# Two scan steps to one GpSimd product, and the next B rows queued one step earlier

## The chip, the cores and the metric

The kernel runs on one core of a Trainium2 chip. Its five engines work side by side, each through its own queue in order: TensorE (PE in the profile, PEld for its weight loads), VectorE (DVE), ScalarE (ACT), GpSimd (POOL) and SyncE (SP), which issues most of the DMAs. The metric is device time in microseconds (us). The median of four runs before the change is 2376.67 us (2375.16 to 2380.18).

## The reference

Input is x of shape (4, 256, 32, 32), 1024 positions for each of four images. A metaformer layer is computed: a channel norm, then four Mamba branches of 64 channels each (inner width 128, 16 states), gates and depthwise convolutions along the positions, attention with eight heads, a second norm with a 3x3 depthwise convolution, and after that a mixture of eight experts with two experts a token. What matters here is the selective scan, for each image, branch, inner channel d and state s:

```
dA = jnp.exp(dt[..., None] * A)
dBu = (dt * u)[..., None] * Bm[:, :, None, :]
def step(h, inp):
    dA_t, dBu_t, C_t = inp
    h = dA_t * h + dBu_t
    return (h, jnp.einsum('bds,bs->bd', h, C_t))
```

The scan runs over the 1024 positions; y is the sum over the 16 states of h times C.

## The kernel before

Images b, branches n and halves h of 512 positions make 4 x 4 x 2 = 32 *parts*, in that order (`parts`, L678). A part has 128 x 16 recurrences of length 512. They are laid on 128 partitions in 16 *steps*: step i = 4q + g takes the channels 32g to 32g+31 and the states 4q to 4q+3. Four steps with the same q are a *block* here; they share B rows and C rows.

For one step, ACT makes the decay dA = exp(dt x A) from `dts` (`decay`, L604), DVE makes the inflow dBu = (dt u) x B (`inflow`, L612), with B's rows in a PSUM bank, and DVE runs the recurrence (`step`, L623) with one scan instruction, out of PSUM and SBUF into an SBUF tile hs. In the first half (h = 0) POOL copies hs's last column into `last` (L627), from which the second half's scan starts. POOL then multiplies hs by C's rows in place (L628). PE sums the four states of a channel with a matmul against `quads` into yp (`sums_of`, L634), one block at a time.

B's rows, spread over 128 partitions, are also made by PE: `spread_b` (L592) issues four matmuls (eight instructions in the profile) with a column of the projection broadcast as weights; it needs u and a PSUM bank. The last step of a block writes its inflow over those rows. C's rows come by DMA (`spread_c`, L586), as dt and dt u do for the four channel groups (`spread_dt`, L567).

`scan` (L710) emits one step. Its order is written out by hand: at the block's third step (g == 2) the next block's `spread_b`; then things of the previous part (`before`: last sums at step 1, `gather` at 3, `project_out` at 6, `add_skip` at 8), things of the next part (`behind`: its dt at steps 0 to 5, its DMAs at 10 to 14, its first `spread_b` at 14), and the next branch's projections (`group`: for instance `project_u` at steps 9 and 10 of the first half); then, at g == 1, `sums_of` for the block before; then the decay three steps ahead, the inflow one step ahead, and the step itself. Each engine does its work in the order in which it was emitted.

After each step comes one `beat`, which advances side tasks by a little: the next image's norm, the convolutions of the image before (`convolutions`, during the first half of an image's parts), and after the fourth part of an image attention of the image before, in which the scan stands still until attention's last tiles. `resume` then takes the scan up again while `joined` (the attention output and fc products, L378), `around` and `sent_off` (routing, with POOL's row scatters at L1692) run in the beats. Expert tiles are a side task from the last part on, and the rest of them follow.

SBUF tiles come from pools of numbered slots: `act4` has 7 slots of 4 KB a partition (u, z, the norm's rows and others), `act2` has 17 of 2 KB (decays, hs, softplus's two, y, and in attention the exponentials e, four a key tile). PSUM has eight banks of 512 columns, one pool for all. A new tile takes a freed slot, and its first writer waits for the old tile's last users.

Of the kernel before, what the change touches and what calls it, by code (L numbers as in the profile page):

```python
# [9 lines left out]
F32 = mybir.dt.float32  # L10
AF = mybir.ActivationFunctionType
ALU = mybir.AluOpType
AX = mybir.AxisListType

P = 128
# [4 lines left out]
HALF = 512  # L20
# [52 lines left out]
def network(  # L73
# [27 lines left out]
    nc = tc.nc  # L101
# [42 lines left out]
    with tc.tile_pool(name="w_conv", bufs=1) as wp, tc.tile_pool(  # L144
        name="act8", bufs=8
    ) as act8, tc.tile_pool(name="act4", bufs=7) as act4, tc.tile_pool(
        name="act2", bufs=17
    ) as act2, tc.tile_pool(name="steps", bufs=2) as actd, tc.tile_pool(
        name="steps4", bufs=6
    ) as acts, tc.tile_pool(name="rows", bufs=3) as actc, tc.tile_pool(  # L150
        name="small", bufs=1
    ) as small, tc.tile_pool(
        name="spread", bufs=2, space=bass.MemoryType.DRAM
# [126 lines left out]
        GD, GS = DIN // 32, DS // 4  # L280
# [71 lines left out]
        def a4(name):  # L352
            return act4.tile([P, N], F32, tag="a4", name=name)

        def a2(name, rows=P):
            return act2.tile([rows, HALF], F32, tag="a2", name=name)
# [144 lines left out]
        T = {}  # L501
# [114 lines left out]
        def step(b, n, h, i):  # L616
            q, g = divmod(i, GD)
            dBu = T.pop((b, n, h, "dBu", i))
            hs = T[b, n, h, "hs", i] = a2(f"hs_{b}_{n}_{h}_{i}")
            if h == 0 and i == 0:  # L620
                T[b, n, "last"] = small.tile([P, NSTEP], F32, tag="last", name=f"last_{b}_{n}", bufs=2)
            last = T[b, n, "last"][:, i : i + 1]
            nc.vector.tensor_tensor_scan(  # L623
                hs, T[b, n, h, "dA", i], dBu, 0.0 if h == 0 else last, ALU.mult, ALU.add
            )
            if h == 0:
                nc.gpsimd.tensor_copy(last, hs[:, HALF - 1 : HALF])  # L627
            nc.gpsimd.tensor_tensor(hs, hs, T[b, n, h, "cs", q], ALU.mult)  # L628

# [21 lines left out]
        def add_skip(b, n, h):  # L651
# [14 lines left out]
            0: [(project_dt,)], 2: [(softplus,)], 4: [(sum_dt,)], 5: [(times_u,)],  # L666
            10: [(spread_dt, 0)], 11: [(spread_dt, 1)], 13: [(spread_dt, 2), (spread_c, 0)],
            14: [(spread_b, 0), (spread_dt, 3)],
        }
# [40 lines left out]
        def scan(at, i, stop):  # L710

            b, n, h = parts[at]
            q, g = divmod(i, GD)
            if g == 2 and q + 1 < GS:
                spread_b(b, n, h, q + 1)
# [216 lines left out]
        def attention(b):  # L932
# [12 lines left out]
            def logits(g, h, kt):  # L945
# [3 lines left out]
                for i in range(4):  # L949
# [4 lines left out]
                    if shifted:  # L954
# [3 lines left out]
                        )  # L958
                es = [a2(f"e_{b}_{g}_{h}_{kt}_{i}") for i in range(4)]
                for i in range(4):  # L960
# [455 lines left out]
class Experts:  # L1416
# [11 lines left out]
    T = 256  # L1428
# [649 lines left out]
```

## Time and profile before

| | before |
|---|---|
| median of four runs | 2376.67 us |
| the profiled execution | 2375.53 us, span 2373.8 us |
| PE, DVE, ACT, POOL busy | 2086.4, 1579.4, 1188.0, 1102.1 us |
| L628, products with C | 512 of 1327 ns |
| L627, copies of the last column | 256 of 236 ns |
| L623, scans | 512, 1207 ns for h = 0 and 1268 ns for h = 1 |
| L612, inflows | 512 of 674 to 678 ns |

In lines of the waits the columns are: engine, line and output that waited, what it waited for, us in total, times, longest. In lines of groups they are: line, engine, operation, output and inputs, shapes, count, then busy us and mean ns, then idle time before them and who ended it. In lines in order of time: start, duration, engine, line, operation, count, and in brackets the idle time before. PE's instructions are pipelined, so a group of them counts as busy a little beyond its last issue.

### The profile page before, as it was taken

What the parts mean: (1) busy time and instruction counts of PE and PEld (TensorE: products, weight loads), DVE (VectorE), ACT (ScalarE), POOL (GpSimd) and SP (SyncE); (2) the same over time, 40 slices, a digit from 0 to 9 for tenths busy, and PEclk for the clock granted to TensorE, in tenths of its full rate; (3) what the DMA queues carried; (4) which work ended last, traced back from release to release, by engine and by line L of the source; (5) the groups of instructions that cost most, each with busy time, mean ns of one, the idle gap of its engine ahead of it and who ended that gap; (6) DMA issues with size and microseconds to landing.
All of it is one profiled execution on the core that took longest, in us unless ns stands there. A gap on an engine that the chain in (4) does not pass through costs nothing. (4 is left out here: it accounts for less than half of the span.)

```text
span 2373.8 us, 28321 instructions
## 1 busy us (share of the span) xinstructions
PE 2086.4 (88%) x8810; PEld 926.9 (39%) x8810; DVE 1579.4 (67%) x2255; ACT 1188.0 (50%) x2013; POOL 1102.1 (46%) x1185
## 2 busy tenths in 40 slices
PE   7778877999887899987779999768999999999995
PEld 2112111332211232322113323205652578788884
DVE  3989999756798888689797876987344164211111
ACT  3554555477656368764264775415258443222221
POOL 0778888612688650565876115571140012422221
PEclk7988998999998999998789999679999999999997
DMA  2454443301343330233433102443340155777764
GB/s 85 118 141 110 110 109 76 88 26 36 87 104 93 74 75 28 57 87 94 115 78 77 32 23 54 104 141 115 80 134 1 43 182 171 230 203 196 197 190 153
DMA packets 155022, 244.33 MB, mean 103 GB/s; under 512 B 34212, under 2 KB 103492, under 8 KB 154856
## 3 DMA queue, kind: packets, MB, share of 16 engines
q1 hardware_dynamic: 135680, 217.07, 32.9%
q0 software_dynamic: 13264, 17.85, 3.9%
q10 hardware_dynamic: 5912, 7.45, 0.9%
q8 instruction: 74, 1.21, 0.2%
q14 instruction: 92, 0.75, 0.1%
HBM read 141.17 MB, written 33.98 MB: 74 GB/s over the span
## 5 line engine op out<-in xcount | busy, mean ns | idle before, releaser
L628 POOL TENSOR_TENSOR hs<-hs,cs 128x512 f32<-128x512 f32 x512 | 678.1, 1327 | 157.4 <-DVE hs L623 92.0
L634 PE MATMUL yp<-hs,quads 128*32 128x512 f32 x1024 | 374.1, 664 | 180.1 <-POOL hs L628 132.5
L604 ACT ACTIVATE dA<-dts,A 128x512 f32<-128x512 f32 x512 | 341.1, 712 | 179.6 <-DMA dts<-dt 127.2
L1945 POOL DMA_INDIRECT Y<-ys,dest x70 | 114.0, 1629 | 535.5 <-DVE ys L1939 528.8
L612 DVE TENSOR_TENSOR dBu<-dts,bs 128x512 f32<-128x512 f32 x384 | 259.9, 678 | 141.5 <-PE bs L596 133.9
L961 ACT ACTIVATE e<-st 128x512 f32<-128x512 f32 x512 | 263.1, 607 | 81.4 <-PE st L951 68.6
L1924 ACT ACTIVATE hs<-h,b 128x256 f32<-128x256 f32 x280 | 115.8, 472 | 341.3 <-PE h L1919 151.7
L1929 PE MATMUL y<-w,hs 128*128 128x256 f32 x1120 | 258.2, 382 | 6.4 <-ACT hs L1924 6.4
L1919 PE MATMUL h<-xT,w 128*128 128x256 f32 x1120 | 252.6, 382 | 1.8 <-DVE xT L1897 1.8
L623 DVE TENSOR_TENSOR_SCAN hs<-dA,last,dBu 128x512 f32<-128x512 f32 x192 | 243.4, 1268 | 0.3
L623 DVE TENSOR_TENSOR_SCAN hs<-dA,dBu 128x512 f32<-128x512 f32 x192 | 231.7, 1207 | 11.7 <-PE av L971 9.8
L627 POOL COPY last<-hs 128x1 f32<-128x1 f32 x256 | 60.4, 236 | 369.2 <-DVE hs L623 364.5
L634 PEld LDWEIGHTS yp<-hs,quads 128*32 128x32 f32 x1024 | 51.7, 112 | 455.1 <-POOL hs L628 319.0
L1919 PEld LDWEIGHTS h<-xT,w 128*128 128x128 f32 x1120 | 213.6, 191 | 39.8 <-issue 7.8
L1929 PEld LDWEIGHTS y<-w,hs 128*128 128x128 f32 x1120 | 211.3, 192 | 42.6 <-issue 8.2
L596 PE MATMUL bs<-u,xpwT_s 128*32 128x512 f32 x1024 | 225.2, 685 | 0.0
L1897 DVE COPY xT<-xp 128x512 f32<-128x512 f32 x35 | 24.2, 691 | 289.4 <-PE xp L1896 289.4
L1003 DVE TENSOR_TENSOR e<-e,e 128x512 f32<-128x512 f32 x256 | 169.7, 724 | 64.6 <-ACT e L961 30.2
L951 PE MATMUL st<-qk 32*128 32x512 f32 x1024 | 192.1, 651 | 7.7 <-ACT e L961 6.1
L993 PE MATMUL av<-e,v 128*32 128x512 f32 x1024 | 144.9, 627 | 0.0
L512 PE MATMUL up<-xn,inwk 64*128 64x512 f32 x256 | 127.7, 641 | 3.4 <-DVE hs L623 3.4
L951 PEld LDWEIGHTS st<-qk 32*128 32x128 f32 x1024 | 68.8, 186 | 129.6 <-issue 87.5
(279 smaller groups left out, 2691.6 us busy)
## 6 DMA issues: line engine op xcount, KB each, us to landing
w<-in_W_dram SPq DMA_DIRECT2D x136, 512.0 KB
dts<-dt SPq DMA_DIRECT2D x512, 128.0 KB
cs<-cd SPq DMA_DIRECT2D x512, 64.0 KB
xs<-XS SPq DMA_DIRECT2D x35, 260.0 KB
b<-in_b_dram SPq DMA_DIRECT2D x35, 128.0 KB
xn<-in_x_dram SPq DMA_DIRECT2D x8, 512.0 KB
XL<-xl SPq DMA_DIRECT2D x8, 512.0 KB
xl<-XL SPq DMA_DIRECT2D x4, 1024.0 KB
```

What stands on the lines that cost most here:

```text
L596: nc.tensor.matmul(bs[r], xpwT_s[:, n, s : s + 1].to_broadcast([P, 32]), T[b, n, "u"][:, half(h)], start=True, stop=True,)
L604: nc.scalar.activation(dA, T[b, n, h, "dts", g][:, 0, :], AF.Exp, scale=A[:, g, n, q : q + 1])
L612: nc.vector.tensor_tensor(dBu, T[b, n, h, "dts", g][:, 1, :], T[b, n, h, "bs", q], ALU.mult)
L623: nc.vector.tensor_tensor_scan(hs, T[b, n, h, "dA", i], dBu, 0.0 if h == 0 else last, ALU.mult, ALU.add)
L628: nc.gpsimd.tensor_tensor(hs, hs, T[b, n, h, "cs", q], ALU.mult)
L634: nc.tensor.matmul(T[b, n, h, "yp"][ts(g, 32)], quads, T[b, n, h, "hs", q * GD + g], start=(q == 0), stop=(q == GS - 1),)
L951: nc.tensor.matmul(sts[i], k[r, ts(kt, P)], q[r, half(h)], start=True, stop=not shifted)
L961: nc.scalar.activation(es[i], sts[i], AF.Exp, scale=1.0 / HD**0.5)
L993: nc.tensor.matmul(accs[0][ts(i, HD)], v8[:, kt, ts(4 * g + i, HD)], es[i], start=(kt == 0), stop=(kt == NK - 1),)
L1003: nc.vector.tensor_tensor(first[i], first[i], es[i], ALU.add)
L1919: nc.tensor.matmul(hp[:, i, :], w1(c, k), xT[:, c, :], start=(c == 0), stop=(c == NC2 - 1))
L1929: nc.tensor.matmul(yp[:, ts(t, C)], hs[:, k, ts(t, P)], w2(k), start=(k == 0), stop=(k == NHC - 1))
```

## The change

The two steps 2k and 2k+1 write their states into the two halves of one 4 KB tile from `act4`. At the even step only the scan is issued. At the odd step POOL copies the two last columns with one instruction (first half only) and multiplies both states by C's rows with one instruction of 1024 columns, in which the C rows are read twice. `spread_b` for the next block is emitted at the block's second step, ahead of that step's `sums_of`; a part's first `spread_b` at step 13 of the part before, ahead of the sums there. `act4` has 11 slots, `act2` 9. In attention the exponentials of even key tiles lie in pairs in `act4`.

```
-    ) as act8, tc.tile_pool(name="act4", bufs=7) as act4, tc.tile_pool(
-        name="act2", bufs=17
+    ) as act8, tc.tile_pool(name="act4", bufs=11) as act4, tc.tile_pool(
+        name="act2", bufs=9
...
+        def pair(name):
+            return act4.tile([P, 2, HALF], F32, tag="a4", name=name)
...
-            hs = T[b, n, h, "hs", i] = a2(f"hs_{b}_{n}_{h}_{i}")
+            if i % 2 == 0:
+                T[b, n, h, "two"] = pair(f"hs_{b}_{n}_{h}_{i}")
+            two = T[b, n, h, "two"]
+            hs = T[b, n, h, "hs", i] = two[:, i % 2, :]
...
+            if i % 2 == 0:
+                return
             if h == 0:
-                nc.gpsimd.tensor_copy(last, hs[:, HALF - 1 : HALF])
-            nc.gpsimd.tensor_tensor(hs, hs, T[b, n, h, "cs", q], ALU.mult)
+                nc.gpsimd.tensor_copy(
+                    T[b, n, "last"][:, i - 1 : i + 1].rearrange("p (g a) -> p g a", a=1),
+                    two[:, :, HALF - 1 : HALF],
+                )
+            nc.gpsimd.tensor_tensor(
+                two, two,
+                T[b, n, h, "cs", q].rearrange("p (a x) -> p a x", a=1).to_broadcast([P, 2, HALF]),
+                ALU.mult,
+            )
...
-            10: [(spread_dt, 0)], 11: [(spread_dt, 1)], 13: [(spread_dt, 2), (spread_c, 0)],
-            14: [(spread_b, 0), (spread_dt, 3)],
+            10: [(spread_dt, 0)], 11: [(spread_dt, 1)],
+            13: [(spread_b, 0), (spread_dt, 2), (spread_c, 0)], 14: [(spread_dt, 3)],
...
-            if g == 2 and q + 1 < GS:
+            if g == 1 and q + 1 < GS:
                 spread_b(b, n, h, q + 1)
...
-                es = [a2(f"e_{b}_{g}_{h}_{kt}_{i}") for i in range(4)]
+                if kt % 2 == 0:
+                    two = [pair(f"e_{b}_{g}_{h}_{kt}_{i}") for i in range(2)]
+                    es = [two[i // 2][:, i % 2, :] for i in range(4)]
+                else:
+                    es = [a2(f"e_{b}_{g}_{h}_{kt}_{i}") for i in range(4)]
```

## The prediction

> **What bounds the kernel now.** I read the page's slices first, then the waits by total, then windows by stage, then DVE's instructions in order of time where it had waited. In this execution the scan's first step starts at 59.8 us, its last ends at 1590, and the mixture of experts fills the rest.
>
> ```profile
> span 2373.8 us, 28321 instructions
> PE   7778877999887899987779999768999999999995
> DVE  3989999756798888689797876987344164211111
> POOL 0778888612688650565876115571140012422221
> ```
>
> The slices change hands: VectorE (DVE) is full in slices 4 to 6 and 12, TensorE (PE) in 9, 10, 15, 16 and 22, and from slice 28 on PE alone works. GpSimd (POOL) never fills a slice. Windows on one part of the scan each, and on the stretch around image 0's attention, sharpen this (columns: PE, weight loads, DVE, ACT, POOL busy, with counts, then clock and DMA).
>
> ```profile
> 655.50:684.10 28.60, 24.83 (x89) 6.70 (x88) 28.60 (x35) 17.39 (x26) 26.14 (x36) 1.00 0.43 103
> 401.40:443.80 42.40, 40.70 (x133) 14.68 (x136) 33.98 (x42) 16.39 (x25) 28.24 (x36) 0.94 0.30 73
> 443.80:570.90 127.10, 126.74 (x748) 39.59 (x744) 85.28 (x110) 95.30 (x182) 37.67 (x30) 1.00 0.16 45
> 570.90:623.60 52.70, 51.03 (x172) 16.07 (x170) 32.08 (x39) 32.06 (x53) 25.01 (x34) 0.97 0.23 56
> 1143.80:1196.40 52.60, 38.17 (x120) 9.21 (x116) 35.69 (x39) 25.05 (x34) 44.62 (x64) 0.81 0.43 117
> ```
>
> The reader is to see three regimes. A plain part has DVE busy for all of its 28.60 us. From 401 to 624 PE is busy for 218.5 of 222.2 us. In the last window nobody is full, though POOL comes nearest. What DVE loses in the scan is one wait above all:
>
> ```profile
> DVE dBu L612 <- PE bs L596: 133.9, 38, 13.9
> DVE y L641 <- PE yp L634: 18.2, 6, 7.5
> ```
>
> and PE's own largest idle time is for POOL's products, which stand before those B rows in its queue:
>
> ```profile
> PE yp L634 <- POOL hs L628: 132.5, 122, 6.3
> ```
>
> One case, PE and DVE in order of time:
>
> ```profile
> 1011.99 1.07 PE L634 MATMUL yp<-hs,quads 128*32 128x512 f32 x8
> 1012.99 1.98 PE L378 MATMUL fc<-xloc,fcT_s 128*128 128x512 f32 x4
> 1014.81 1.88 PE L378 MATMUL fc<-xglo,fcT_s 128*128 128x512 f32 x4
> 1016.62 1.06 PE L596 MATMUL bs<-u,xpwT_s 128*32 128x512 f32 x8
> 1017.75 0.69 DVE L612 TENSOR_TENSOR dBu<-dts,bs 128x512 f32<-128x512 f32 x1 [11.60 <-PE bs L596]
> ```
>
> The B rows come out only after the sums and one side task of the beat between: 4.6 us of PE's queue.
>
> **Edit 1, B rows a step earlier.** It removes nothing: the same eight matmuls a block (1.06 us) move ahead of the previous block's sums (another 1.06 us and any wait for POOL) and ahead of one beat of side work. No DMA moves with them, SP's order is the same, and POOL issues nothing for them; they need only u and a PSUM bank, held one step longer. The 133.9 us fall into four lots, by the single waits in DVE's timeline.
> - Not touched: 6.9 us (the first block) and 2.5 us (two resumptions after attention): 9.4.
> - Where PE has room: 3.15 + 1.36 (at 74 and 83 us), 6.05 (152), 1.02 (357), 4.63 (752), and 5.72 + 6.20 + 4.26 (1166 to 1194): 32.4. The first two and the 1.02 go whole (5.5). The 6.05 is partly taken back, because 9 us later DVE waits 2.48 for a decay: 3.5. The 4.63 goes whole, as its rows stood behind a gate product that waited 2.48 us for ACT. Of the last three I take 10: POOL is busy for 44.6 of that part's 52.6 us and edit 2 takes 6 off it, so the part stays at 42 or so. Sum 23.6.
> - Where PE is full (parts 10 to 12 of image 1's scan and their likes in the next two): 27.6 + 28.4 + 30.7 = 86.6. Rows that come earlier there only put other PE work later, so what counts is the last wait of the stretch, after which DVE is the bound again. That one ends sooner by what the rows pass: sums and an fc product, 4.6 us, in two images, and 6.3 in the third, where a variance product (1.8 us) stands between too: 15.5. PE's idle time in such a stretch is 1.7 + 0.4 + 1.7 = 3.7 us, of which I take 1 an image: 18.5 in all.
> - Waits below 1 us: 5.5 together, of which I take 1.
>
> Bounds: nothing of the full-PE lot and half of the other lots (15 us), to all of 32.4 + 5.5 and 25 of the 86.6 (63). A loss by the bank: if PE had to wait for DVE to free it, the sums behind would stand too, but these wait for POOL until after that same scan step (PE's idle time that ended with a scan of DVE is some 8 us in all), so 0 to 8; I take 0.
>
> **Edit 2, one product for two steps.** It removes 512 products of 128x512 (L628, mean 1.327 us) and 256 copies (L627, 0.236), and adds 256 products of 128x1024 and 128 copies of two columns. The nearest row for the product is the gate's on the same engine:
>
> ```profile
> L818 POOL TENSOR_TENSOR xm<-g,xm 128x1024 f32<-128x1024 f32 x8 | 17.9, 2239 | 21.5 <-ACT g L810 21.5
> ```
>
> whose shortest took 1.99 and whose longest 2.74 us. It reads no operand twice as the new one does with C; the bounds are 1.99 and, with a pass for each half, 2.65, and I take 2.1, near the undisturbed gate rows. A copy lies between 0.18 and 0.37; I take 0.2. POOL then saves about 0.4 us a pair in h=1 and 0.7 to 0.8 in h=0, some 150 us of 930 in the scan. Nearly all of it is worth nothing, for DVE covers it; if POOL did bind, it would count in full. It counts in the part at 1143 us (in the 10 above) and at the end of the scan, where DVE waits 7.47 us for the last sums behind 4.5 to 7 us of POOL's lag: 3.
>
> The added wait: the even step's product now stands until the odd scan has ended. Behind it on POOL are that copy, dt's two products, the square and row-scatter work; PE's sums wait for it. With POOL undisturbed a block's last product ended 1.4 to 1.6 us after its scan and will end 2.2 to 2.5 after. The sums are read by the part's gather alone, three steps (5.2 us) later, and PE needs 1.1 us between, so 0.8 us is hidden; and the B rows no longer stand behind them. Without that cover it would cost 0.8 x 128 blocks, 102 us. Attention's four last gathers follow eight av matmuls that PE does meanwhile: 0 to 4 us, I take 0.
>
> A loss that the rows do show: DVE operations with two SBUF operands and POOL's instructions keep each other out. At L411 1.25 us becomes 2.07, at L1638 0.38 becomes 1.35. Summed over the scan, such operations of DVE outside attention exceed the shortest of their kind by some 26 us. A POOL instruction in the way is met in proportion to its length and costs in proportion again: 2 x 1.27^2 = 3.2 against 2.1^2 = 4.4, a third more. Up to 10 us; half of them stand where DVE binds: 6. The Trainium skill, SBUF — State Buffer, section "SBUF: two separate sides", speaks against the change in the same way: the pair of ports is a lock held for the whole instruction. By a lock that cost its full length at each meeting the loss would be 10 rather than 6.
>
> **Edit 3, pools.** Pairs and half of attention's e tiles move into 11 slots of 4 KB; 9 of 2 KB stay for decays and the rest. Live in the scan are 4 decays and at most 4 others, and 4 (u, z) + 3 pairs with up to 3 others. Decays had waited 19.1 us for sums and 14.9 for dt, on ACT, which is idle for 12 us or more of most parts. In attention an odd key tile's e takes slots freed two to four tiles before, where it was three. Between -2 and +8 us over three attentions; I take +2. For the experts I count nothing: 264.5 us of DVE and 725.7 of PE in their 773 us, and no tile of theirs loses a slot that it used.
>
> **Sum.** 23.6 + 18.5 + 1 + 3 - 6 - 2 = 38 us. The execution took 2375.53 (span 2373.8), the median is 2376.67, 1.1 more: 2376.7 - 38 = 2339.
>
> **Rivals.**
> - POOL becomes the bound (slower). The second operand's repeated half may cost more than any row shows. A plain h=0 part lasts 28.6 us; POOL has three other products there (3.8) and eight pairs, so it binds from (28.6 - 3.8) / 8 - 0.26 = 2.84 us a product. At 3.3 us each of 16 such parts grows by 3.7: +59, 2339 + 59 = 2398; from about 3.14 us on it eats the gain. For: nothing has this form. Against: 2.84 is over the longest gate product, which was disturbed.
> - The waits only move. PE is 98% busy where 86.6 of the 133.9 us lie; if the rows are then late for a bank or the sums for a slot, the 18.5 vanish and the others halve: 38 - 18.5 - 12 = 8, so 2369. For: DVE waits there while PE works. Against: PE falls idle for 6 to 13 us in the parts on either side.
> - More goes than I count: the scan's DVE waits mostly vanish, 63 + 5 - 3: 2312. For: nobody is full at 1143 to 1196. Against: PE's 218.5 us.
>
> **How the numbers follow.** My case has 0.60 (its own range 2322 to 2358), moved waits 0.18 (half of it within 0.2%, about 4.8 us, which is what a measurement here tells from no change), POOL as bound 0.17, more 0.05. Faster 0.60 + 0.05 + 0.09 = 0.74, same 0.09, slower 0.17. From 2310 to 2384 leaves out most of the second and the last rival, about 0.16.
>
> **What would show it.** DVE's wait for bs falls from 133.9 to between 60 and 85 us, with the three long ones near 7 and none at 752 or 1194; L628's group is 256 of about 2.1 us; POOL's busy time drops by about 150; plain parts keep their 28.6 us. PE's wait for POOL products may even rise. I am wrong if the product's mean is over 2.84, if DVE waits for yp or hs in plain parts, or if attention's 127 us grow by more than 3.

## The result and the profile after

The changed kernel takes 2385.03 us in the median of 44 runs, the kernel before 2379.84 in 70 runs beside it. The ratio is 1.0014 with a 95% interval of 1.0002 to 1.0026: within 0.2%, and if anything slower. Forecast was 2339 us, with a range from 2310 to 2384. The profiled execution took 2383.16 us. The 44 runs lie in groups some 10 us apart, about 2364, 2375, 2385 and 2395, and the longer a group's time, the lower its mean TensorE clock (0.898, 0.894, 0.890, 0.885 in the median). The kernel before has 0.93.

From the page of the changed kernel: span, busy times, and the slices.

```profile
span 2381.3 us, 27847 instructions
...
PE 2040.9 (86%) x8810; PEld 923.9 (39%) x8810; DVE 1599.8 (67%) x2255; ACT 1190.6 (50%) x2013; POOL 1017.4 (43%) x801
...
PE   7767777999967799987679999648999999999995
...
DVE  3889899865898988789978777987344164211111
...
POOL 0676676631676750356766205571140011422221
PEclk7786788999987899998589999758999999999997
```

POOL is relieved, by 85 us (1102.1 to 1017.4) where some 150 were forecast. The line to look at is the last one: before, PEclk's first seven slices read 7988998, now 7786788.

The waits of the changed kernel by total (engine, line, output, what it waited for, us, times, longest):

```profile
PE yp L649 <- POOL hs L639: 140.7, 73, 5.3
...
DVE y L656 <- PE yp L649: 29.2, 8, 8.1
DVE dBu L615 <- PE bs L599: 28.0, 10, 6.6
DVE dBu L615 <- ACT xc L1108: 25.7, 6, 7.0
```

DVE's wait for B rows fell from 133.9 to 28.0 us, further than the 60 to 85 forecast. In part the wait changed its name: 25.7 us are now waits for ACT's reads of fc products, which stand in PE's full stretches beside the B rows. PE's wait for products grew little in sum (132.5 to 140.7) but comes in 73 pieces where there were 122, so the mean wait grows from 1.1 to 1.9 us.

The windows of the changed kernel that answer those shown of before, each on its own part of the scan (PE, weight loads, DVE, ACT, POOL busy, then clock and DMA). The first two are the scan's first part and a plain part of image 0; then come the plain part shown of before, parts 10, 11 and 12, and the part that had started at 1143.8.

```profile
60.10:98.50 38.40, 32.38 (x90) 8.01 (x82) 27.69 (x33) 20.36 (x31) 20.38 (x18) 0.64 0.39 100
211.40:250.40 39.00, 34.78 (x92) 8.45 (x88) 29.30 (x36) 14.57 (x21) 23.67 (x20) 0.62 0.34 82
667.70:696.90 29.20, 23.95 (x96) 5.71 (x90) 28.77 (x35) 17.50 (x26) 23.78 (x20) 0.94 0.42 103
420.00:461.50 41.50, 39.49 (x121) 14.45 (x122) 35.17 (x42) 15.81 (x24) 24.47 (x20) 0.92 0.31 76
461.50:588.50 127.00, 126.74 (x753) 40.57 (x753) 85.69 (x110) 96.08 (x183) 37.80 (x22) 1.00 0.16 45
588.50:635.00 46.50, 44.36 (x160) 14.98 (x159) 33.14 (x39) 28.66 (x46) 21.26 (x18) 1.00 0.25 63
1158.80:1207.40 48.60, 36.86 (x114) 8.77 (x108) 37.38 (x39) 21.93 (x31) 41.18 (x47) 0.65 0.47 128
```

The part after attention went from 52.7 to 46.5 us, its like in the next two images by 5.1 and 8.0, the part at 1143.8 from 52.6 to 48.6: the gains are there. Against them stand two parts that nobody had on the list. The part at 211.4 lasts 39.0 us instead of 29.1, the first one 38.4 instead of 33.0, and their clock is 0.62 and 0.64 where before it was 0.94 and 0.90. The same two parts in the kernel before:

```profile
205.20:234.30 29.10, 26.57 (x90) 6.86 (x88) 29.00 (x36) 14.71 (x21) 26.36 (x36) 0.94 0.41 101
59.80:92.80 33.00, 25.24 (x84) 6.26 (x76) 27.65 (x32) 20.49 (x32) 23.89 (x34) 0.90 0.49 120
```

The place that the prediction showed, image 1's part after attention, PE and DVE of the changed kernel in order of time:

```profile
1020.73 0.70 DVE L615 TENSOR_TENSOR dBu<-dts,bs 128x512 f32<-128x512 f32 x1 [5.85 <-ACT xc L1108]
...
1024.43 1.88 PE L381 MATMUL fc<-xglo,fcT_s 128*128 128x512 f32 x4
1026.24 1.06 PE L599 MATMUL bs<-u,xpwT_s 128*32 128x512 f32 x8
1027.12 1.04 PE L649 MATMUL yp<-hs,quads 128*32 128x512 f32 x8
1027.43 0.69 DVE L615 TENSOR_TENSOR dBu<-dts,bs 128x512 f32<-128x512 f32 x1 [3.17 <-ACT xc L1108]
```

The B rows now stand ahead of the sums. Where DVE had waited 11.60 us for them it waits 5.85 and 3.17, and the last thing that it waits for is ACT.

And the groups on POOL in the changed kernel:

```profile
L639 POOL TENSOR_TENSOR hs<-hs,cs 128x1024 f32<-128x1024 f32 x256 | 617.2, 2412 | 174.1 <-DVE hs L629 93.6 <-DMA dts<-dt 19.8 <-issue 15.9
...
L635 POOL COPY last<-hs 128x2 f32<-128x2 f32 x128 | 33.0, 258 | 379.3 <-DVE hs L629 359.2 <-DMA cs<-cd 20.1
...
L833 POOL TENSOR_TENSOR xm<-g,xm 128x1024 f32<-128x1024 f32 x8 | 17.6, 2214 | 22.0 <-DVE xi L1161 20.1 <-ACT g L825 1.9
```

The pair product has a mean of 2.41 us (shortest 2.34), not 2.1.

### The profile page after: what moved, and what is told of

Its sections match the earlier page's. It is cut to its first block, busy times and chain, and to the rows that moved or that the text cites. A ratio compares the mean times of both kernels' runs of the same rounds, so it can differ in the third digit from the quotient of the medians.

```text
span 2381.3 us, 27847 instructions
## 1 busy us (share of the span) xinstructions
PE 2040.9 (86%) x8810; PEld 923.9 (39%) x8810; DVE 1599.8 (67%) x2255; ACT 1190.6 (50%) x2013; POOL 1017.4 (43%) x801
## 5 line engine op out<-in xcount | busy, mean ns | idle before, releaser
L639 POOL TENSOR_TENSOR hs<-hs,cs 128x1024 f32<-128x1024 f32 x256 | 617.2, 2412 | 174.1 <-DVE hs L629 93.6
L649 PE MATMUL yp<-hs,quads 128*32 128x512 f32 x1024 | 272.7, 726 | 187.0 <-POOL hs L639 140.7
L629 DVE TENSOR_TENSOR_SCAN hs<-dA,dBu 128x512 f32<-128x512 f32 x192 | 231.8, 1207 | 1.9 <-ACT dA L607 1.8
L1948 PEld LDWEIGHTS y<-w,hs 128*128 128x128 f32 x1120 | 211.4, 192 | 42.3 <-issue 8.2
L599 PE MATMUL bs<-u,xpwT_s 128*32 128x512 f32 x1024 | 175.5, 709 | 44.6 <-DVE hs L629 30.9
L635 POOL COPY last<-hs 128x2 f32<-128x2 f32 x128 | 33.0, 258 | 379.3 <-DVE hs L629 359.2
L649 PEld LDWEIGHTS yp<-hs,quads 128*32 128x32 f32 x1024 | 44.0, 120 | 382.2 <-POOL hs L639 241.3
L515 PE MATMUL up<-xn,inwk 64*128 64x512 f32 x256 | 147.8, 727 | 1.7 <-DVE hs L629 1.6
```

Of the source, the lines that this page charges most:

```text
L515: nc.tensor.matmul(up, inwk[rows, c, k, :], XN[b][rows, c, ds(k + h * HALF, HALF)], start=(k == 0), stop=(k == KC - 1),)
L599: nc.tensor.matmul(bs[r], xpwT_s[:, n, s : s + 1].to_broadcast([P, 32]), T[b, n, "u"][:, half(h)], start=True, stop=True,)
L629: nc.vector.tensor_tensor_scan(hs, T[b, n, h, "dA", i], dBu, 0.0 if h == 0 else last, ALU.mult, ALU.add)
L639: nc.gpsimd.tensor_tensor(two, two, T[b, n, h, "cs", q].rearrange("p (a x) -> p a x", a=1).to_broadcast([P, 2, HALF]), ALU.mult,)
L649: nc.tensor.matmul(T[b, n, h, "yp"][ts(g, 32)], quads, T[b, n, h, "hs", q * GD + g], start=(q == 0), stop=(q == GS - 1),)
L1948: nc.tensor.matmul(yp[:, ts(t, C)], hs[:, k, ts(t, P)], w2(k), start=(k == 0), stop=(k == NHC - 1))
```

## Experiments

### The three edits apart

The first question is which edit gives and which takes. Four kernels, beside the changed one, take the edits apart. First the earlier B rows alone, in the kernel before:

```
-            if g == 2 and q + 1 < GS:
+            if g == 1 and q + 1 < GS:
...
-            10: [(spread_dt, 0)], 11: [(spread_dt, 1)], 13: [(spread_dt, 2), (spread_c, 0)],
-            14: [(spread_b, 0), (spread_dt, 3)],
+            10: [(spread_dt, 0)], 11: [(spread_dt, 1)],
+            13: [(spread_b, 0), (spread_dt, 2), (spread_c, 0)], 14: [(spread_dt, 3)],
```

> The kernel before with the earlier B rows alone: single products of 512 columns, the old pools. Theory 'clock': the gain of the B rows is real, and what eats it in the changed kernel is that the pair products let TensorE idle 3 us and more at a time, after which its clock is halved. Then this kernel keeps the old one's clock (0.92 to 0.94 over the span, no half-speed piece of 27 us in the scan after its first part), DVE's wait for B rows falls from 133.9 to 30 to 55 us, parts 12, 20 and 28 shorten by 4 to 8 us each, and the time is 15 to 30 us below the kernel before (ratio 0.988 to 0.994). Rival 'bank': rows that are taken a step earlier hold a PSUM bank, and DVE's inflow then waits for ACT to free another; the gain is taken back whatever the products are. Then DVE's waits for ACT's reads of PSUM appear here as in the changed kernel (25 to 50 us) and the time is within 5 us of before.

Measured: 2353.01 us against 2380.5, ratio 0.9875 (0.9853 to 0.9896). The span's clock is 0.927, parts 12, 20 and 28 are 5.6, 5.7 and 7.9 us shorter. DVE's wait is this line:

```profile
DVE dBu L612 <- PE bs L596: 35.6, 9, 10.0
```

The rows' gain is real without the rest. (Kernels of different comparisons are set against each other by their ratios from here on, because the kernel before itself took 2370 to 2380 us beside them; 1% is 23.8 us.)

The reverse, the changed kernel's pairs and pools with the rows at their old place:

```
-            if g == 1 and q + 1 < GS:
+            if g == 2 and q + 1 < GS:
...
-            13: [(spread_b, 0), (spread_dt, 2), (spread_c, 0)], 14: [(spread_dt, 3)],
+            13: [(spread_dt, 2), (spread_c, 0)], 14: [(spread_b, 0), (spread_dt, 3)],
```

> The changed kernel with the B rows back at their old place: pair products, pair copies and pools alone. Theory 'clock': slower than the kernel before by 15 to 30 us (ratio 1.006 to 1.013), clock over the span at or below 0.90, with long half-speed pieces in the plain parts; DVE's wait for B rows stays at 110 to 150 us. Rival 'bank': within 5 us of before or faster, clock as before.

Measured: 2411.76 us, ratio 1.0112 (1.0082 to 1.0141), clock 0.899. Plain parts last 1 to 2 us more, because the B rows stand behind sums that wait for a pair.

Then pair tiles, pools and early rows, but a product and a copy for each step as before (against the changed kernel, as all that follow unless they say otherwise):

```
-            if i % 2 == 0:
-                return
             if h == 0:
-                nc.gpsimd.tensor_copy(
-                    T[b, n, "last"][:, i - 1 : i + 1].rearrange("p (g a) -> p g a", a=1),
-                    two[:, :, HALF - 1 : HALF],
-                )
-            nc.gpsimd.tensor_tensor(
-                two, two,
-                T[b, n, h, "cs", q].rearrange("p (a x) -> p a x", a=1).to_broadcast([P, 2, HALF]),
-                ALU.mult,
-            )
+                nc.gpsimd.tensor_copy(last, hs[:, HALF - 1 : HALF])
+            nc.gpsimd.tensor_tensor(hs, hs, T[b, n, h, "cs", q], ALU.mult)
```

> The changed kernel with one product and one copy for each step again; early B rows, pair tiles and pools stay. Theory 'clock': as with the earlier rows alone, within 5 us of it, clock 0.92 to 0.94. If the pools cost something, it is slower than the earlier rows alone by that, up to 8 us, and it lies in the three attentions. Rival 'bank': as the changed kernel, within 5 us.

Measured: 2342.46 us, ratio 0.9826 (0.9802 to 0.9851), clock 0.921. The expectation allowed for a cost of the pools; they gave 0.49% more, 12 us. And they do so by themselves, with single products and the rows back as in the diff above:

> The kernel before with the pools and pair tiles of the changed one alone: B rows late, a product and a copy for each step. With the early rows the pools were worth 10.5 us (2353.0 to 2342.5). Theory 'slots by themselves': the smaller pool of decays costs nothing and the pairs' slots help whatever the rows do: 8 to 13 us below the kernel before. Rival 'slots for the early rows': they matter only where the early rows let ACT run ahead; within 4 us of the kernel before.

Measured: 2368.61 us against 2378.39, ratio 0.9953 (0.9935 to 0.9970). ACT's wait of 19.1 us for PE's sums ahead of its decays is gone from the list there, since states no longer take the decays' slots. But ACT's idle time ahead of decays grew as a whole, from 179.6 to 228.3 us, with 56.1 of it now waits for DVE's scans. So that the pools gain is measured, and why is not shown.

So the change is, nearly, a sum of three effects. The early rows are worth 1.25% alone, 1.27% with the new pools (0.9953 to 0.9826) and 0.98% under pairs (1.0112 to 1.0014). The pools are worth 0.47% alone and 0.49% with the rows. The pair product costs 1.88% with early rows (0.9826 to 1.0014) and 1.59% without (0.9953 to 1.0112). In us: -30 for the rows, -12 for the pools, +45 for the pair; by the order in which they are taken, the rows and the pair differ by up to 7 us. The rest of the experiments ask why the pair is so dear.

### TensorE's clock

The clock record of the changed kernel falls in pieces, either full or half speed. Three windows of the changed kernel around the long part at 211.4 us, cut where the record changes:

```profile
213.40:220.20 6.80, 4.00 (x18) 0.71 (x18) 6.80 (x9) 2.77 (x5) 5.49 (x5) 1.00 0.11 39
220.20:247.50 27.30, 26.43 (x56) 6.98 (x56) 18.70 (x22) 8.20 (x11) 15.87 (x13) 0.50 0.45 107
247.50:254.40 6.90, 4.50 (x28) 0.83 (x20) 5.80 (x7) 6.86 (x12) 3.44 (x3) 0.99 0.06 16
```

And PE in order of time there, the changed kernel:

```profile
217.01 1.05 PE L649 MATMUL yp<-hs,quads 128*32 128x512 f32 x4
221.07 1.92 PE L649 MATMUL yp<-hs,quads 128*32 128x512 f32 x4 [3.00 <-POOL hs L639]
222.92 1.97 PE L664 MATMUL op<-y,moutT_s 128*64 128x512 f32 x2
224.82 2.07 PE L523 MATMUL zp<-xn,inwT_s 64*128 64x512 f32 x2
226.82 1.93 PE L599 MATMUL bs<-u,xpwT_s 128*32 128x512 f32 x8
228.68 7.19 PE L515 MATMUL up<-xn,inwk 64*128 64x512 f32 x8
```

PE does half of a block's sums, waits 3.00 us for the second pair's product, and in that wait the clock halves. It stays halved for 27.3 us although PE is then busy for 26.4 of them. The up projection's eight matmuls take 7.19 us where before they took 3.59 to 3.70, and DVE waits 6.63 us for B rows behind them. The first part of the scan has the same piece from 66.6 to 93.9 us; there the wait was one of 3.47 us. In the kernel before, PE's longest idle time in this part was 1.65 us and the clock was full from 208.6 to 331 us.

The Trainium skill, TensorE: Matmul & The Clock Gate, section "Part 1: The HAM clock gate", has the two speeds and a window of 3.4 us, with half speed after an idle window and full speed after a busy one. The two speeds and the step of 3.4 us agree with these records (27.3 us are eight such steps). That a whole idle window is needed, or that one busy window ends the half speed, does not: the longest wait in the part at 211.4 us was 3.00 us, with PE busy for 4.00 of the 6.80 us ahead of the piece, and PE was 97% busy for eight steps at half speed.

The test fills the wait with useless work in image 0 and changes nothing else. After a block's second sum PE makes the B rows of two blocks on once more:

```
+        def spread_again(b, n, h, q):
+            b, n, h = parts[parts.index((b, n, h)) + q // GS]
+            bs = T.get((b, n, h, "bs", q % GS))
+            if bs is not None:
+                for i, r in enumerate(states):
+                    s = DTR + 4 * (q % GS) + i
+                    nc.tensor.matmul(
+                        bs[r], xpwT_s[:, n, s : s + 1].to_broadcast([P, 32]),
+                        T[b, n, "u"][:, half(h)], start=True, stop=True,
+                    )
...
                     start=(q == 0), stop=(q == GS - 1),
                 )
+                if g == 1 and b == 0:
+                    spread_again(b, n, h, q + 2)
```

> The changed kernel with more work: in image 0's eight parts PE makes the next block's B rows a second time, between the second and the third sum, in the wait for the last pair's product (four matmuls, about 1 us at full clock, some 30 times). Theory 'clock': the filled waits keep the clock up; in parts 0 to 7 it rises from a mean of 0.75 to 0.85 or more, the part at 208 us falls from 39.0 to about 30 us and the first part from 38.4 to about 33, and the time is 8 to 15 us below the changed kernel's. Without that theory 30 us more of PE work can only keep the parts as long or make them longer: 0 to 10 us above the changed kernel's.

Measured: 2367.33 us, ratio 0.9948 (0.9929 to 0.9967), 0.66% or 16 us below the changed kernel, with 256 more matmul instructions. The two parts in the filled kernel's windows:

```profile
203.10:232.20 29.10, 26.19 (x130) 7.19 (x124) 29.00 (x36) 14.60 (x20) 23.82 (x20) 0.97 0.41 100
61.40:89.80 28.40, 24.70 (x122) 6.61 (x114) 27.56 (x33) 20.31 (x31) 20.53 (x18) 0.94 0.53 128
```

They are back at 29.1 and 28.4 us, the clock at 0.97 and 0.94, and no half-speed piece of over 14 us is left in image 0. More work on PE made the kernel faster. The edit removes no work and no wait by itself, and the clock is what moved: over image 0's eight parts it rose from 0.75 to 0.91.

A second way out is to let the sums come when their products are ready:

```
-            if g == 1 and q > 0:
+            if g == 2 and q > 0:
                 sums_of(b, n, h, q - 1)
```

> The changed kernel with a block's sums one step later (emitted at g == 2 instead of g == 1), when the last pair's product has ended. Theory 'the wait stands in PE's queue': sums that find their pair ready let the work behind them go, so the pieces of idle time get shorter (the longest in the plain parts from 3.0 to below 2 us), TensorE's clock rises above 0.90, the parts at 420, 812 and 1252 us lose the 1.7 us each that they gained on the kernel with single products, and the time is 10 to 25 us below the changed kernel's 2385. Rival 'PE's idle time is what it is': PE has 4 to 11 us of it in each plain part wherever it stands, and the clock falls all the same: within 6 us of the changed kernel.

Measured: 2344.80 us, ratio 0.9853 (0.9829 to 0.9878): 1.61% or 38 us below the changed kernel, more than expected. But the clock is 0.896 and did not rise as the theory had it. The mean clock is not the price. What counts is whether a long half-speed piece meets the up projection. Four of the parts with up projections (at 60, 211, 280 and 668 us in the changed kernel), in the traces of all 20 kernels, give 80 cases. In 16 of them a half-speed piece of 24 to 31 us covers the up matmuls, and those parts last 34 to 39 us. In the other 64, half speed meets at most 1 us of them, and the parts last 27 to 33 us. Here the two parts take 27.6 and 29.1 us, while the part after the second has its usual 29.6 us at a clock of 0.77, since PE is busy for 18 us of it alone:

```profile
229.50:259.10 29.60, 17.98 (x70) 2.91 (x70) 29.60 (x36) 13.90 (x22) 22.72 (x12) 0.77 0.42 107
```

Later sums with single products:

> Single products, early B rows and the new pools, and the sums a step later: the candidate for the best version. If the sums' wait in PE's queue costs there too (PE waits 70.5 us for products in the kernel with single products, 2.6 us ahead of the parts in which it is full), the time is 3 to 10 us below that kernel's 2342, with PE's wait for products below 30 us. If not, within 3 us of it.

Measured: 2336.02 us, ratio 0.9809 (0.9784 to 0.9834), 0.17% or 4 us below single products with the sums at the old place, which the intervals do not tell from nothing. One part, though, was caught again, in the profile of that kernel:

```profile
198.00:232.10 34.10, 30.94 (x80) 8.01 (x74) 29.10 (x36) 15.07 (x21) 26.23 (x36) 0.61 0.37 93
207.30:231.20 23.90, 23.41 (x57) 6.56 (x56) 18.90 (x22) 10.70 (x15) 17.64 (x24) 0.50 0.49 122
```

It had no idle time over 1.7 us in that part, so a long wait isn't the only way into a half-speed piece. Filling was tried on this kernel too, with the same edit as above:

> The best so far (single products, early B rows, new pools, sums a step later: 2336.0) with image 0's B rows made a second time between the sums. Its profile had one half-speed piece of 24 us at 207 us in which PE was 97% busy, and that part took 34.1 us where 29.0 is its usual length. Theory 'clock': the added work keeps the clock up there, and the time is 2328 to 2334. Rival 'PE work is a cost': 2336 to 2345.

Measured: 2352.92 us, ratio 0.9885 (0.9854 to 0.9917), 18 us worse and slower than either theory had it. The piece was gone, but the second writing of the rows now stood behind the later sums, and DVE waited for it (the kernel with filled and later sums):

```profile
DVE dBu L615 <- PE yp L651: 28.2, 10, 10.2
```

What worked with single products is the old place for image 0 alone:

```
-            if g == 1 and q > 0:
+            if g == (2 if b else 1) and q > 0:
```

> Single products, early B rows, new pools, sums a step later in images 1 to 3 only. With the later sums everywhere a half-speed piece of 24 us at 207 us met the up projection and its part took 34.1 us; with the sums at g == 1 that part took 29.0 and no such piece lay in image 0. Theory 'clock': no half-speed piece of over 14 us in image 0, that part back at 29, and 2 to 5 us below the 2336 of later sums everywhere (parts 0 and 2 give back some 3 to 6 us, part 4 and the next ones win 5 to 9). Rival: the piece comes by chance whatever the sums do, 2336 to 2342.

Measured: 2329.05 us, ratio 0.9780 (0.9759 to 0.9802). The part at 202 us has 29.0 us again. One half-speed piece of 17 us is left in image 0, against the expectation, but it lies from 187 to 204 us, where PE is idle for 15.6 of its part's 42.4 us, and that part is no longer than with early sums. The gain on later sums everywhere is 0.29%, 7 us, though the two intervals overlap.

### Length and lateness

A pair is both later (the even step's product waits for the odd step) and longer. Two instructions at the odd step keep the first and drop the second:

```
-            nc.gpsimd.tensor_tensor(
-                two, two,
-                T[b, n, h, "cs", q].rearrange("p (a x) -> p a x", a=1).to_broadcast([P, 2, HALF]),
-                ALU.mult,
-            )
+            for k in range(2):
+                nc.gpsimd.tensor_tensor(two[:, k, :], two[:, k, :], T[b, n, h, "cs", q], ALU.mult)
```

> The changed kernel with the pair's product as two instructions of 512 columns, both issued at the odd step. It keeps the lateness (the even step waits for the odd one) and drops the long instruction. The kernel with single products at each step took 2342, the changed one 2385; what lies between is split here. Theory 'length': the excess of DVE's operations with two SBUF operands (44 us in the scan with pair products, 32 with single ones) falls back to 30 to 34, and with it 8 to 12 us of time. Theory 'lateness': the last product of a block still ends 2.5 us or more after its scan, so PE's waits for products stay at 130 to 150 us and the clock at or below 0.905. If both hold, the time is 2365 to 2377; if length were all, 2340 to 2348; if lateness were all, 2380 to 2390.

Measured: 2351.05 us, ratio 0.9884 (0.9862 to 0.9906), clock 0.929. Lateness is not the main cost. Two products of 1.25 us end later after the odd scan than one of 2.34 (all at their shortest), yet 1.30% or 31 of the 45 us are gone. A sum can run between the two products, so PE waits in shorter pieces (115.1 us in 116 waits; in the parts from 201 to 319 us none is over 1.8 us), and the two long parts are back at 28.5 and 29.3 us. DVE's operations that read SBUF alone (attention's products left out) exceed the shortest of their kind over the scan by some 36 us here, 44 in the changed kernel, 32 with single products and 30 before. So most of the cost is that of the single long instruction. The clock and what POOL keeps out of DVE are the two ways that the traces show. The other 0.58% or 14 us on single products may be lateness or the shared copy; no run tells them apart.

### What a 1024-column product costs

Does the second read of C's rows cost? One kernel multiplies the pair by itself, one by u's 1024 columns, one has C first. In the first two C's rows do not enter y.

```
-                two, two,
-                T[b, n, h, "cs", q].rearrange("p (a x) -> p a x", a=1).to_broadcast([P, 2, HALF]),
-                ALU.mult,
+                two, two, two, ALU.mult,
```

```
+                two, two, T[b, n, "u"].rearrange("p (a x) -> p a x", a=2), ALU.mult,
```

```
+                two,
+                T[b, n, h, "cs", q].rearrange("p (a x) -> p a x", a=1).to_broadcast([P, 2, HALF]),
+                two, ALU.mult,
```

> The changed kernel with the pair multiplied by itself in place of C's rows (so y is not the reference's): what does a 1024-column product cost without an operand that is read twice? The gate's products of plain 1024-column operands took 1.99 us at their shortest, the pair product 2.34. Theory 'the repeat costs': the shortest falls to 1.95 to 2.1 us. Rival 'two different states': 2.3 us or more, and the repeat is not the reason.

> The changed kernel with the pair multiplied by the 1024 columns of u in place of C's rows (y is not the reference's; C's rows are still fetched): two different tiles, none read twice. The pair by itself took 1.95 us in the mean (shortest 1.89), the pair by C read twice 2.41 (2.34). Theory 'the repeated read costs': 2.0 to 2.1 us in the mean, as the undisturbed gate products, and a time of 2340 to 2355, as the one look at the pair by itself gave 2345. Rival 'a second tile costs': 2.35 to 2.45 us and a time near the changed kernel's 2385.

> The changed kernel with the operands of the pair product exchanged: C's rows, read twice, come first. If the price lies with the second operand's repeat alone, the mean falls from 2.41 to about 2.0 us and the time to 2340 to 2355; if it lies with a repeated read in whichever place, 2.35 to 2.45 us and 2375 to 2390.

The groups of the three kernels, in this order:

```profile
L639 POOL TENSOR_TENSOR hs<-hs 128x1024 f32<-128x1024 f32 x256 | 499.7, 1952 | 210.6 <-DVE hs L629 166.2 <-PE qkp L381 10.0 <-DVE count L1686 5.9
```

```profile
L639 POOL TENSOR_TENSOR hs<-hs,u 128x1024 f32<-128x1024 f32 x256 | 617.8, 2414 | 172.4 <-DVE hs L629 117.1 <-PE qkp L381 10.0 <-PE yp L647 7.5
```

The third has a mean of 2.41 us too. Their times are 2345.2 (one run), 2385.06 (ratio 1.0016, 0.9994 to 1.0037) and 2383.87 us (1.0009, 0.9982 to 1.0037). The repeat costs nothing, in either place (2.412 us in the mean with it, 2.414 without). A second tile costs 0.45 us; and with a product of 1.95 in place of 2.41 the whole kernel was 1.3% below the kernel before in its one run.

That left the gate's products, with two different tiles and yet 2.0 us for the first channel half (2.35 for the second). Their rows lie in a padded tile, one column and 1027 columns from its start. So C's rows were shifted by one column in their tile (five one-column constants share a tile to make room), and later by two and three:

```
-            t = T[b, n, h, "cs", q] = actc.tile([P, HALF], F32, tag="cs", name=f"cs_{b}_{n}_{h}_{q}")
+            t = T[b, n, h, "cs", q] = actc.tile([P, HALF + 1], F32, tag="cs", name=f"cs_{b}_{n}_{h}_{q}")[:, 1:]
```

> The changed kernel with C's rows one column (4 bytes) further on in their tile; five one-column constants share a tile to make room. The gate's products of two different 1024-column tiles come in two kinds, 1.99 to 2.02 us for the first channel half and 2.34 to 2.37 for the second, and these differ in where a row starts in the padded tile. The pair product took 2.34 at its shortest with any two different tiles, 1.89 with one. Theory 'places': two operands whose rows start at like places disturb each other; shifted, the mean falls from 2.41 to 2.0 to 2.1 us and the time to 2340 to 2355. Rival 'not the start of the row': 2.35 to 2.45 us, time 2375 to 2390, and the gate's two kinds stay unexplained.

> The changed kernel with C's rows two columns (8 bytes) further on. If any unlike start will do, the shortest pair product is 1.99 to 2.01 us as with one column; if the start must be odd in columns or lie within 4 bytes, 2.33 to 2.36.

> The changed kernel with C's rows three columns (12 bytes) further on. The gate's second product starts three columns past a multiple of 4 KB in its padded tile and took 2.34 us or more; if the start alone decided, this one takes 2.33 to 2.36; if any unlike start will do, 1.99 to 2.01, and the gate's second half has another reason.

The groups with one, two and three columns:

```profile
L640 POOL TENSOR_TENSOR hs<-hs,cs 128x1024 f32<-128x1024 f32 x256 | 526.7, 2058 | 205.1 <-DVE hs L630 123.9 <-DMA dts<-dt 20.9 <-DMA cs<-cd 12.5
```

```profile
L640 POOL TENSOR_TENSOR hs<-hs,cs 128x1024 f32<-128x1024 f32 x256 | 525.9, 2055 | 204.3 <-DVE hs L630 123.4 <-DMA dts<-dt 15.6 <-PE rp L382 10.8
```

```profile
L640 POOL TENSOR_TENSOR hs<-hs,cs 128x1024 f32<-128x1024 f32 x256 | 617.5, 2413 | 174.0 <-DVE hs L630 95.1 <-DMA dts<-dt 20.5 <-issue 15.9
```

The shortest are 1.989, 1.983 and 2.337 us. One or two columns take 0.35 us off every product, three take nothing, and three is what the gate's slow half is off by a multiple of 4 KB. With one column the time is 2360.26 us, ratio 0.9912 (0.9881 to 0.9944), 1.02% or 24 us below the changed kernel and above the 2340 to 2355 expected: its profile still has two half-speed pieces, whose parts (at 260 and 654 us) last 8.7 and 9.4 us longer than in the changed kernel. With two it was 2343.35 and with three 2384.47 us, one run each beside 2369.96.

The same shift on the best kernel so far, single products:

> The best so far (single products, early B rows, new pools, sums a step later from image 1 on: 2329.05) with C's rows one column further on in their tile. For the pair that took 0.35 us off the shortest product (2.34 to 1.99). If the place of the rows counts per column, a single product falls from 1.25 to about 1.08 us, POOL's busy time by some 90 us, and the time by 2 to 10 us (2319 to 2327), since POOL is nowhere the bound but its operations keep DVE's out. If it concerns long operations alone, 1.25 us and 2329 as before.

Measured: 2306.71 us, ratio 0.9738 (0.9707 to 0.9768): the fastest of all. By the ratios the shift is worth 0.42% or 10 us, with intervals that touch, so the size is loose. The profiles say less: the two spans differ by 15 us, but only 3 of it lie up to the end of the scan. The other 12 lie in the stretch after the scan, where at most the last such product is left. It took 774 to 775 us here and in the kernels with two and three columns, the three that were timed beside a kernel before of 2369.96 us; in every other profile it took 782 to 787 us. The product of 512 columns falls from 1.251 to 1.080 us at its shortest:

```profile
L635 POOL TENSOR_TENSOR hs<-hs,cs 128x512 f32<-128x512 f32 x512 | 582.7, 1139 | 195.9 <-DVE hs L630 126.0 <-issue 7.9 <-DMA cs<-cd 7.7
```

Last, pairs with both repairs, sums a step later and C shifted by one column:

> The changed kernel's pairs with both repairs: sums a step later (2344.8 with that alone) and C's rows one column further on (2360.3 with that alone). With single products the same repairs gave 2306.7. If pairs were only badly placed, they now come out level with single products or ahead, 2300 to 2310, since POOL issues half as many instructions. If the pair itself keeps a price (DVE's operations shut out for 2.0 us at a time and not 1.1, sums that come four at a time), 2315 to 2335.

Measured: 2330.78 us, ratio 0.9795 (0.9770 to 0.9819). By the ratios the pair is still 0.57% or 14 us dearer than single products with the same shift, whose sums come later from image 1 on only (with single products that difference alone was 7 us). In the profiles the scan ends only 4 us later; the other 13 us lie in the stretch after it, which was 12 us shorter in that one group of kernels. So with both repairs the pair gains nothing on single products, and what it still costs lies somewhere from 4 to 14 us. DVE's excess is some 37 us against 30, and in the parts in which PE is full its idle time comes as one wait of 4.7 to 4.8 us where single products have 2.6.

## Why the prediction was wrong

The step that failed is the added wait of edit 2, taken at 0. The pair's product costs 45 us on single products, and the largest piece of it that the traces show is PE's clock, halved after the waits that the pair makes: 17.3 us in two parts. The product's price and the sign of the pools were wrong beside it.

**Edit 1, B rows a step earlier: right mechanism, 43.1 forecast, 30 measured alone.** The two lots changed places. In the full-PE stretches the forecast was 18.5, and the rows alone shorten parts 10 to 12, 18 to 20 and 26 to 28 by 9.3, 11.3 and 11.6 us: 32. The step "what counts is the last wait of the stretch" gave too little: all three parts of each stretch got shorter, not its end alone. Where PE has room 23.6 was forecast, and parts 0, 2, 8, 16 and 24 together give nothing (-3.4, -1.2, +4.9, +2.6, -2.3). The wait at 752 us was to go whole; in its place stand a wait of 3.12 us for ACT's g and one of 2.0 for rows. With the new pools the five parts win 11.2. Three parts that were not on the list, at 375, 767 and 1207 us in the changed kernel, grew by 3.1 each; the rows make 1.3 of it and with the new pools 2.5, without any pair. So the prediction's waits did move there, as the second rival had it for PE's full stretches.

**Edit 2, the product: taken at 2.1 us, measured 2.41.** The step that failed here is "near the undisturbed gate rows". The gate's eight products were two kinds, 1.99 to 2.1 and 2.35 to 2.74, and the slow kind was read as disturbed. It was the kind that the new product belongs to. The shifts by one and two columns show that for the scan's product the start of its operands' rows decides between the two. The upper bound 2.65 held for the mean. The price of 2.41 is also why POOL's busy time fell by 85 us and not by 150. The Trainium skill, GPSIMD Engine Reference, section "3.1 Elementwise — side-by-side cycle accounting", has about 2.6 cycles for an element of an operation with two inputs, at 1.2 GHz; the estimate from it is 1024 x 2.6 / 1.2 = 2.2 us and an issue time, near the measured 2.34 and no limit, as 1.98 shows.

**Edit 2, the added wait: taken at 0, it was the largest loss.** "A block's last product ... 0.8 us is hidden" was true for the sums, and DVE never waits for yp in a plain part. What the working left out is PE's clock. The prediction counted PE's idle time in sums and as room; the pair gathers it into waits of 3.0 and 3.5 us, the clock halves, and the two parts at 60 and 211 us lose 17.3 us against single products (38.4 for 31.0 and 39.0 for 29.1). Filling the wait brought both parts back, and so did the product in two instructions, as late as the pair. "Plain parts keep their 28.6 us" failed there. The four last gathers of attention, "0 to 4, I take 0", belong here too: in the nine parts around attention the pair costs 11.5 us against single products.

**Edit 2, POOL and DVE keep each other out: the rule was too steep, its duration too short.** Of 26 us of excess a third more, up to 10, was worked out at 2.1 us, and half of it taken as binding, which is 5 and was put at 6. (Of its two rows L1638 reads one wide tile, not two.) At 2.41 the same rule gives 5.8 against 3.2, or 21. Measured are 12 (44 for 32 with single products). How much of the 12 stands where DVE binds was not told apart. The lock that the Trainium skill, SBUF — State Buffer, section "SBUF: two separate sides", describes agrees in kind with these rows (1.25 us that becomes 2.07); its size here (10 in place of 6) is neither confirmed nor excluded.

**Edit 2, last sums: taken as a gain of 3.** The scan's last part is 1.6 us shorter; the rows alone give 0.3 of it.

**Edit 3, the pools: taken as a loss of 2, measured as a gain of 12.** "On ACT, which is idle for 12 us or more" was the reason to count the decays' waits for slots at nothing. The pools that end the wait for sums gain 11 to 12 us, though ACT's idle time ahead of decays grows; what carries the gain stays open.

Put together by the ratios: 1.25% + 0.49% - 1.88% = -0.14%, which is the changed kernel's 1.0014, as it must be when each step is measured from the one before. Rivals: POOL did not become the bound, the product stayed below 2.84. None of the three had the clock in it, by which here a wait on an engine with room cost time. The forecast 2339 lies by chance near the 2342.5 of rows and pools without pairs.

**Not settled.** The pair's 45 us can't be cut into exact parts: the clock's 17, DVE's 12 and the full stretches' 11.5 may overlap, and each repair alone (filled wait 16, shift 24, two instructions 31, later sums 38) takes away some of the others. Ahead of 13 of the 16 long pieces counted above stands a wait of 2.7 to 3.5 us. Ahead of the other three (one at 207 us, two in the first part of other kernels) none is over 1.7 us. What all 16 share is that PE was busy for only 0.7 to 1.8 of the 3.4 us before them; whether that share is the rule, and why the half speed then holds, is open. So is why one and two columns help and three do not: the norm's products (xl) read one tile three columns in for the first channel half and yet take 2.0 us, so the start of the rows is not the whole rule. That DVE's new waits for ACT come from the bank that early rows hold was only expected, and no run tests it; they stand in the kernel with single products as well (25.0 us).

## What to carry to other kernels

Idle time on an engine with room can cost time when it is gathered into long pieces, as the waits of 3 us on TensorE did here. Before gathering work into larger instructions, look at the longest wait that this makes on TensorE, and at what stands behind it when the clock has halved. Where a row that a price is taken from has two values, find what tells them apart before calling one disturbed. And when an edit bundles three things, time them one by one: here two of them gave 42 us, and the pair took 45.

## What was not expected of the hardware

- The time of the scan's GpSimd product depends on where the rows of its two tiles start. 1024 columns at their shortest: 2.34 us with C's rows at the start of their tile or three columns in, 1.99 and 1.98 with them one or two columns (4 or 8 bytes) in, 1.89 with one tile read for both. 512 columns: 1.251 and, one column in, 1.080 us. One column of padding was worth 24 us with pairs, and 3 us (scan of the profile) to 10 (ratios) with single products.
- TensorE's clock fell to half in waits of 2.7 to 3.5 us and three times without any over 1.7, and then stayed there for 24 to 31 us with PE 93 to 100% busy. Eight matmuls of the up projection took 7.19 us in place of 3.7. One such piece on the wrong spot costs 5 to 10 us, which is near the distance between the groups of the changed kernel's runs. A step of 0.004 in the mean clock is, by an estimate from the span, 2381 x 0.004 x 2 = 19 us more at half speed, about what one piece of 27 us adds to the usual 7. That the groups differ by one such piece fits this and was not traced, since one execution of the changed kernel has a profile.
- The mean clock did not tell the time: ratio 0.9853 at 0.896 with later sums, 0.9875 at 0.927 with early rows alone.
